# Turned tokens in banks of their own, a new order of VectorE's first work, and fillers at the start of a fused attention and FFN kernel

## The chip, the cores and the metric

The kernel runs on one core of a Trainium2 chip. A core has five engines that run their own instruction streams and meet through semaphores: TensorE (PE, matrix products and transposes), VectorE (DVE), ScalarE (ACT), GpSimd (POOL) and SyncE (SP, which here issues most of the DMA transfers). Matrix products are written to PSUM, a small memory of banks; everything else lies in SBUF. The metric is the time of one execution on the device in microseconds (us), the lower the better, given as the median of several runs.

## The reference

The input x has 4 batches of 512 tokens of 256 features, all in fp32. Cut to what matters:

```python
xn = layernorm(x)                              # (4, 512, 256), no gain
# attention block on xn: 16 heads of 128, 4 key/value heads
Q, K, V = xn @ Wq + bq, xn @ Wk + bk, xn @ Wv + bv
attn = softmax(Q K^T / sqrt(128) + causal mask)
y = gelu((attn @ V) @ Wo + bo)                 # exact gelu
s = layernorm(xn + y) * gamma + beta
# FFN on xn: 2 x 1024 hidden features
gate, up = split(xn @ w_gate_up.T)
g = silu((silu(gate) * up) @ w_down.T)
out = x + s * g
```

## The kernel before

Every product is kept close to fp32 by splitting each operand into a high and a low part and adding three products: high by high, high by low, low by high. A split is a copy with rounding (the high part) and a subtraction (the low part). `product` (L251) issues the three matmuls, at L253, L254 and L255 in that order. `split_psum` (L240) splits a PSUM tile, the high part on ACT (L244), the low part on DVE (L245); `split_sbuf` does the same for weights, on the engines that `load_w` is told: L267 and L269 are the high parts on ACT and POOL, L270 the low part.

The work falls into stages.

**Start.** The four 128-token tiles of x[0] are loaded, and with them the columns of the first weight block for FFN feature blocks f = 0 and f = 1 (`st_first`). PE is given 16 transposes of the identity (`warm_up`, L349). For each token tile `moments` takes mean and variance on DVE, `inverse_root` the power of -0.5 on POOL (L362), and `normed` writes xn on DVE (L379) and sends it to DRAM through SP (L382, `fin_dram`). `normed` takes its tile from the pool tag `u`, which has two buffers: the third xn needs the buffer of the first, and so the end of the first one's transfer.

`transposed` (L387) turns two token tiles at a time: four PE transposes (L395), feature half c by token tile k, into one PSUM tile `pxt`, and then for each feature half a split into `xT`. The first weight block is split by `first_hi` (ACT, L337) and `first_lo` (DVE, L341). `behind(key)` puts what is issued inside it after the last instruction noted under that key, in the order of its engine.

**FFN.** `gate_up_product` (L509) multiplies xT of batch b with the gate and up weights of a feature block f: 12 matmuls of 512 columns, and for (b, f) = (0, 0) 24 of 256 columns, the first 256 tokens before the second, so that they can start when only two token tiles are turned. `gate_silu` (ACT, L535), `gate_times_up` (DVE, L538), `inner_hi` (ACT, L545) and `inner_lo` (DVE, L550) make the hidden activations and their split. `down_product` then fills `pd` for each token tile with the down weights `wd` (split by POOL). `gate` (ACT, L572) takes silu of `pd` into a tile of the tag `gate`, which has two buffers; `gate_scaled` (POOL, L577, once each for gamma and beta) and `gate_shifted` (POOL, L581, adds x) prepare what the end needs, and `gate_out` (SP, L584) writes it to `fin_dram`. The activation of gate_3 goes to the buffer of gate_1, and so waits for gate_1's write to land.

Beside it the weights arrive: `load_w` stages each block in one of two buffers, so a block's load waits for the split of the block before the last. `split_group` (L992, L994) loads the query and output weights on ACT's queue, splits them on POOL into `p` tiles and writes the halves to DRAM (`w_dram`, L1000, L1001), from which they are read back in time.

**Attention.** The last FFN batch and 16 phases of attention are recorded by a planner, the class `Order`, whose tasks have costs and fixed keys; all its instructions bear the line L52.

The order of instructions of each engine outside of `Order` is set by the framework's scheduler, from its own model of time, with `behind` as a constraint. An edit at the start can so move instructions further down. Each engine runs its instructions in the order so fixed. DMAs are issued in the order of their queue, SP's or ACT's; semaphores of eight slots are shared by SP's and ACT's transfers in turn, and the issue of one may wait for the landing of an earlier one.

Of the kernel before, what the change touches and what calls it, by code (L numbers as in the profile page):

```python
# [11 lines left out]
F32 = mybir.dt.float32  # L12
# [6 lines left out]
P = 128  # L19
# [162 lines left out]
def kernel(  # L182
# [20 lines left out]
    nc = tc.nc  # L203

    B, L, D = x.shape
# [3 lines left out]
    G = H // KV  # L209
    INTER = wdT.shape[0]  # L210
    NT = L // P
    ND = D // P
# [6 lines left out]
    work = ctx.enter_context(tc.tile_pool(name="work", bufs=2))  # L219
    rows = ctx.enter_context(tc.tile_pool(name="rows", bufs=4))  # L220
    psum = ctx.enter_context(tc.tile_pool(name="psum", bufs=2, space=PSUM))
    dram = ctx.enter_context(tc.tile_pool(name="dram", bufs=1, space=DRAM))

    pe, dve, act, pool, sp = nc.tensor, nc.vector, nc.scalar, nc.gpsimd, nc.sync
    latest = {}

    @contextmanager
    def behind(*keys):

        with ExitStack() as stack:  # L230
            for k in keys:
                for ins in latest[k]:
                    stack.enter_context(tc.issue_after(ins.ins))
            yield


    def pair(tag, bufs, name, n=512):
        return work.tile([P, 2, n], F32R, tag=tag, bufs=bufs, name=name)

    def split_psum(dst, src, bias=None):  # L240

        hi, lo = dst[:, 0], dst[:, 1]
        if bias is None:
            first = nc.scalar.copy(hi, src)  # L244
            second = nc.vector.tensor_tensor(lo, src, hi.bitcast(F32), ALU.subtract)  # L245
        else:
            first = nc.scalar.activation(hi, src, AF.Identity, bias=bias)
            second = nc.vector.scalar_tensor_tensor(lo, src, bias, hi.bitcast(F32), ALU.add, ALU.subtract)
        return first, second

    def product(out_ap, lhs, rhs, first, last, **kw):  # L251

        pe.matmul(out_ap, lhs[0], rhs[0], start=first, stop=False, **kw)  # L253
        pe.matmul(out_ap, lhs[0], rhs[1], start=False, stop=False, **kw)  # L254
        pe.matmul(out_ap, lhs[1], rhs[0], start=False, stop=last, **kw)  # L255


    mhalf = small.tile([P, NT], F32, name="mhalf")
# [34 lines left out]
    ident = const.tile([P, P], F32, name="ident")  # L293
# [6 lines left out]
    def load_x(b):  # L300
        if b < 2:
            t = work.tile([P, NT, D], F32, tag="xT", bufs=2, name=f"x_{b}")
        else:
            t = p_tiles[NT - 1][:, ts(b - 2, 2)].rearrange("p a n -> p (a n)").rearrange("p (t d) -> p t d", d=D)
        if b > 0:
            nc.sync.dma_start(t, x[b].rearrange("(t p) d -> p t d", p=P))
        return t
# [7 lines left out]
    xs = {0: load_x(0)}  # L315
# [13 lines left out]
    def first_parts(f):  # L329
        v = w_first.rearrange("p s (c u f n) -> p s c u f n", c=ND, u=2, f=2)  # L330
        for c in range(ND):
            yield v[:, 0, c, :, f], v[:, 1, c, :, f], st_first[:, c, :, f]

    def first_hi(f):

        for hi, _, st in first_parts(f):
            nc.scalar.copy(hi, st)  # L337

    def first_lo(f):
        for hi, lo, st in first_parts(f):  # L340
            nc.vector.tensor_tensor(lo, st, hi.bitcast(F32), ALU.subtract)  # L341


    make_identity(nc, ident)


    warm_up = psum.tile([P, P], F32, tag="y0", bufs=1, name="warm_up")
# [4 lines left out]
    mv = small.tile([P, B, NT, 2], F32, name="mv")  # L352
    rstd = small.tile([P, B, NT], F32, name="rstd")

    def moments(dst, src, name):
        st = rows.tile([P, nc.vector.BN_STATS_DIM], F32, tag="st", bufs=4, name=name)
        dve.bn_stats(st, src)
        dve.bn_aggr(dst, st)

    def inverse_root(dst, var):  # L360
        dve.tensor_scalar(dst, var, EPS, 1.0, ALU.add, ALU.mult)
        pool.tensor_tensor(dst, dst, mhalf[:, : dst.shape[1]], ALU.pow)  # L362

    def stats(b, t0, t1):
        for t in range(t0, t1):
            moments(mv[:, b, t], xs[b][:, t], f"st_{b}_{t}")
        inverse_root(rstd[:, b, t0:t1], mv[:, b, t0:t1, 1])
# [7 lines left out]
    w_dram = {(k, g): dram.tile([P, 2, 1024], F32, tag=f"w{k}{g}", name=f"w_dram_{k}{g}") for k in "qo" for g in range(KV)}  # L375

    def normed(b, t):
        xn = work.tile([P, D], F32, tag="u", bufs=2, name=f"xn_{b}_{t}")
        latest["xn"] = (nc.vector.tensor_scalar(  # L379
            xn, xs[b][:, t], mv[:, b, t, 0:1], rstd[:, b, t : t + 1], ALU.subtract, ALU.mult  # L380
        ),)
        nc.sync.dma_start(fin_dram[b][:, t, 0], xn)  # L382
        return xn

    xT = {}

    def transposed(b, t, xn=None):  # L387

        if t == 0:
            xT[b] = [pair("pt", 4, f"xT_{b}_{c}") for c in range(ND)]  # L390
        xn = xn or [normed(b, t), normed(b, t + 1)]
        pt = psum.tile([P, ND, 2, P], F32, tag="s", bufs=2, name=f"pxt_{b}_{t}")
        for c in range(ND):
            for k in range(2):
                nc.tensor.transpose(pt[:, c, k], xn[k][:, ts(c, P)], ident)  # L395
        for c in range(ND):
            dst = xT[b][c][:, :, ds(t * P, 2 * P)]
            latest["xT"] = split_psum(dst, pt[:, c].rearrange("p k q -> p (k q)"))
        if t + 2 == NT:
            for c in range(ND):  # L400
                nc.sync.dma_start(xT_dram[b][:, c], xT[b][c].bitcast(F32))
# [6 lines left out]
    def x_pair(b, c):  # L408
        return xT[b][c][:, 0], xT[b][c][:, 1]

    stats(0, 0, 1)
    stats(0, 1, 2)
    first_hi(0)
    first_xn = [normed(0, t) for t in range(2)]
    with behind("xn"):
        first_lo(0)
        stats(0, 2, 3)
        stats(0, 3, 4)
    transposed(0, 0, first_xn)
    with behind("xT"):  # L420
        first_hi(1)
    transposed(0, 2)
    with behind("xn"):
        first_lo(1)
    wgu = [w_first]


# [40 lines left out]

    banks = [psum.tile([P, L], F32, tag=f"c{r}", bufs=1, name=f"bank{r}") for r in range(G)]

    def h_tiles(b):

# [31 lines left out]
    def gate_up_product(b, f, us=(0, 1)):  # L506
        nonlocal n_ff
        w = wgu[f // 2]
        for u in us:  # L509
            k = n_ff % (G + 2 if b + 1 < B else G)  # L510
            n_ff += 1
            if k < G:
                ps = banks[k]
            else:
                ps = psum.tile([P, L], F32, tag="s", bufs=2, name=f"pg_{b}_{f}_{u}")
            gate_banks.setdefault((b, f), []).append(ps)
        parts = 2 if (b, f) == (0, 0) else 1
        n = L // parts
        for m in range(parts):
            for u in us:  # L520
                for c in range(ND):
                    at = c * 512 + u * 256 + (f % 2) * P
                    hi, lo = x_pair(b, c)
                    product(
                        gate_banks[b, f][u][:, ts(m, n)],
                        (w[:, 0, ds(at, P)], w[:, 1, ds(at, P)]),
                        (hi[:, ts(m, n)], lo[:, ts(m, n)]),
                        m == 0 and c == 0,
                        c == ND - 1,
                        skip_group_check=parts > 1,  # L530
                    )

# [20 lines left out]
    def gate_up(b, f):  # L553
        gate_up_product(b, f)
        gate_silu(b, f)
        gate_times_up(b, f)
        inner_hi(b, f)
        inner_lo(b, f)
# [86 lines left out]
    q0, k0, vr, bank, turned = {}, {}, {}, {}, {}  # L645
# [391 lines left out]
    pe, dve, act, pool, sp = (order.engine(e) for e in (nc.tensor, nc.vector, nc.scalar, nc.gpsimd, nc.sync))  # L1037
# [12 lines left out]
    def group_of(ph):  # L1050
        return divmod(ph, KV)
# [9 lines left out]
    for f in range(NI):  # L1061
        b, key = B - 1, -8.0 + 0.1 * f
        add("Ug", "PE", 1.39, key, lambda b, f: gate_up_product(b, f, (0,)), (b, f), after=[("U", b, f - 1)] + first_queries, takes=BANKS[2 * (f % 2)])
        add("U", "PE", 1.39, key, lambda b, f: gate_up_product(b, f, (1,)), (b, f), after=[("Ug", b, f)], takes=BANKS[2 * (f % 2) + 1])
        add("Us", "ACT", 0.6, key, gate_silu, (b, f), after=[("Ug", b, f)] + first_exps, takes="ctx", mode=2)
        add("Um", "DVE", 0.67, key, gate_times_up, (b, f), after=[("Us", b, f), ("U", b, f)], gives=tuple((t, "U", f) for t in BANKS[2 * (f % 2) :][:2]))
        done = [("D", B - 2, t) for t in range(NT)] if f < 3 else [("U", b, 3)] if f > 3 else []
        add("Uh", "ACT", 0.6, key, inner_hi, (b, f), after=[("Um", b, f), ("Uh", b, f - 1)] + done)
        add("Ul", "DVE", 0.9, key, inner_lo, (b, f), after=[("Uh", b, f)], gives=(("ctx", b, f),))
    order.task(("gb",), "SP", 0.7, -9.0, late_scales, after=[("before",)], takes="ctx", lag=4.5, mode=2)  # L1070
    for b in (B - 2, B - 1):
        e = "POOL" if b + 1 < B else "DVE"
        c = 0.75 if b + 1 < B else 0.35
# [24 lines left out]
    for ph in range(NPH):  # L1098
        b, g = group_of(ph)
# [59 lines left out]
        for i in range(NT):  # L1159
            last = ph + 1 == NPH  # L1160
# [37 lines left out]
        last = ph + 1 == NPH  # L1198
# [47 lines left out]
        if g == KV - 1:  # L1246
# [12 lines left out]
            for t in range(NT):  # L1259
                k = key + (0.1 * (t ^ 2) if late else K["f1"] * t)  # L1260
# [81 lines left out]
```

## Time and profile before

| | |
|---|---|
| median of 3 runs | 621.54 us (620.61 to 622.39) |
| the profiled execution | 621.86 us, span 620.0 us, granted clock 0.994 |
| busy in the span: PE, DVE, ACT, POOL | 608.8, 414.7, 405.5, 452.9 us |
| first transpose of xn on PE, first product | 5.23 us, 6.76 us |
| end of feature blocks 0 and 1 of batch 0 on PE | 17.54 us |
| granted clock of PE from 8.5 to 15.0 us | 0.50 |
| PE idle from 60 to 100, 100 to 140, 140 to 200 us | 1.22, 0.21, 1.10 us |

All times of a profile are counted from the start of the span; the time of the execution is 1.86 us longer than the span. A row of a timeline has the start, the length, the engine, the line of the kernel and the operation with the tiles that it writes and reads, and in brackets how long the engine was idle before it and what released it. The chain of work is followed back from the last instruction: each row has the start and the length, and what the chain passes through there. The rows of windows give each engine's busy time in a stretch, with the number of instructions, then the granted clock, the DMA engines' busy share and their rate.

### The profile page before, as it was taken

What the parts mean: (1) busy time and instruction counts of PE and PEld (TensorE: products, weight loads), DVE (VectorE), ACT (ScalarE), POOL (GpSimd) and SP (SyncE); (2) the same over time, 40 slices, a digit from 0 to 9 for tenths busy, and PEclk for the clock granted to TensorE, in tenths of its full rate; (3) what the DMA queues carried; (4) which work ended last, traced back from release to release, by engine and by line L of the source; (5) the groups of instructions that cost most, each with busy time, mean ns of one, the idle gap of its engine ahead of it and who ended that gap; (6) DMA issues with size and microseconds to landing.
All of it is one profiled execution on the core that took longest, in us unless ns stands there. A gap on an engine that the chain in (4) does not pass through costs nothing.

```text
span 620.0 us, 16073 instructions
## 1 busy us (share of the span) xinstructions
PE 608.8 (98%) x6100; PEld 550.0 (89%) x6100; DVE 414.7 (67%) x1139; ACT 405.5 (65%) x1030; POOL 452.9 (73%) x591
## 2 busy tenths in 40 slices
PE   7999999999999999999999999999999999999997
PEld 6888888898987999899899989898998899998996
DVE  5964545745528876748777774877687569668747
ACT  3542334754349876759888774987796579678762
POOL 2698767493316988739968993896899659888973
PEclk7999999999999999999999999999999999999999
DMA  7764768464597286762786694298396825839562
GB/s 230 254 205 150 271 225 256 169 230 142 138 315 180 69 201 210 181 194 74 256 233 143 268 234 170 59 289 216 121 338 133 263 73 161 236 99 261 140 170 64
DMA packets 86237, 118.10 MB, mean 190 GB/s; under 512 B 5648, under 2 KB 72336, under 8 KB 82064
## 3 DMA queue, kind: packets, MB, share of 16 engines
q1 hardware_dynamic: 81408, 113.93, 62.0%
q10 hardware_dynamic: 4752, 3.15, 1.7%
q8 instruction: 48, 0.79, 0.5%
q14 instruction: 29, 0.24, 0.1%
HBM read 87.70 MB, written 29.36 MB: 189 GB/s over the span
## 4 chain that ended last, share of the span: by engine, by line
PE 80%; POOL 7%; DMA 6%; DVE 4%; issue 1%; ACT 1%; SPq 0%; ACTq 0%; DVEq 0%; POOLq 0%
PE bank L52 42%; PE py L52 14%; PE ps L52 11%; PE pv L52 4%; PE pd L52 3%; PE pk L52 3%; DMA w_dram_o<-p 2%; DVE y L52 1%; POOL w_d L270 1%; DMA st_gu<-in_wguT_dram 1%; DMA st_d<-in_wdT_dram 1%; DMA w_dram_q<-p 1%; DMA fin_dram<-gate 1%; POOL p L52 1%; POOL gate L577 1%
## 5 line engine op out<-in xcount | busy, mean ns | idle before, releaser
L52 POOL TENSOR_SCALAR p<-p,total 128x384 f32<-128x384 f32 (+7 forms) x248 | 119.1, 500 | 28.3 <-DVE total L52 27.4
L52 ACT ACTIVATE p<-p,least 128x192 f32<-128x192 f32 (+15 forms) x256 | 130.6, 512 | 10.7 <-DVE least L52 9.6
L52 POOL TENSOR_TENSOR pT<-u_more,pT 128x512 fp32r<-128x512 f32 x78 | 101.3, 1308 | 26.3 <-ACT pT L52 26.1
L52 PEld LDWEIGHTS bank<-pT,vr 32*128 32x128 f32 x3168 | 113.3, 185 | 6.1 <-issue 1.7
L52 PE MATMUL bank<-pT,vr 32*128 32x256 f32 (+15 forms) x3168 | 118.3, 303 | 0.0
L52 POOL TENSOR_TENSOR pT<-u,pT 128x512 fp32r<-128x512 f32 x82 | 105.6, 1296 | 15.7 <-ACT pT L52 15.5
L52 PE MATMUL py<-w_o,ctxT 128*128 128x256 f32 x768 | 107.0, 285 | 1.3 <-DVE y L52 0.7
L52 PEld LDWEIGHTS py<-w_o,ctxT 128*128 128x128 f32 x768 | 100.9, 191 | 6.6 <-DVE y L52 1.5
L52 DVE CUSTOM_DVE_ANT_0 p<-ps,mask 128x192 f32<-128x192 f32 (+15 forms) x170 | 69.8, 434 | 47.3 <-PE ps L52 46.8
L52 PE MATMUL bank<-xT_again,w_q 128*128 128x512 f32 x384 | 97.4, 394 | 0.8 <-DVE least L52 0.6
L52 PEld LDWEIGHTS bank<-xT_again,w_q 128*128 128x128 f32 x384 | 70.3, 188 | 15.3 <-DVE least L52 1.5
L52 PE MATMUL ps<-kT,qT 128*128 128x352 f32 (+11 forms) x387 | 74.9, 325 | 0.0
L52 ACT ACTIVATE ctxT<-bank,bv_sb 128x512 fp32r<-128x512 f32 (+1 forms) x68 | 42.7, 662 | 48.8 <-PE bank L52 42.6
L52 DVE STREAM_TRANSPOSE u_more<-p 128x512 f32<-128x512 f32 x78 | 53.3, 693 | 21.1 <-POOL pT L52 10.3
L52 DVE STREAM_TRANSPOSE u<-p 128x512 f32<-128x512 f32 x82 | 56.2, 692 | 14.4 <-POOL p L52 8.1
L52 PEld LDWEIGHTS ps<-kT,qT 128*128 128x128 f32 x387 | 60.1, 189 | 5.1 <-issue 0.5
L52 ACT CAST pT<-u_more 128x512 fp32r<-128x512 f32 x78 | 47.6, 618 | 21.9 <-DVE u_more L52 17.4
L52 DVE SCALAR_TENSOR_TENSOR ctxT<-bank,bv_sb,ctxT 128x512 fp32r<-128x512 f32 (+1 forms) x68 | 47.2, 711 | 17.6 <-ACT ctxT L52 17.5
L52 ACT CAST pT<-u 128x512 fp32r<-128x512 f32 x82 | 50.3, 618 | 10.3 <-DVE u L52 9.1
L52 DVE SCALAR_TENSOR_TENSOR qT<-bank,bq_sb,qT 128x384 fp32r<-128x384 f32 x64 | 38.9, 607 | 22.8 <-ACT q L52 20.2
L52 ACT ACTIVATION_READ_ACCUMULATOR p<-p,least 128x1 f32 x256 | 48.1, 188 | 0.0
L52 ACT ACTIVATE qT<-bank,bq_sb 128x384 fp32r<-128x384 f32 x64 | 37.0, 578 | 14.1 <-PE bank L52 13.9
(146 smaller groups left out, 1039.4 us busy)
## 6 DMA issues: line engine op xcount, KB each, us to landing
vr<-v_dram SPq DMA_DIRECT2D x128, 256.0 KB, 5.3
w_q<-w_dram_q SPq DMA_DIRECT2D x15, 1024.0 KB, 7.6
w_o<-w_dram_o SPq DMA_DIRECT2D x15, 1024.0 KB, 9.8
v_dram<-v SPq DMA_DIRECT2D x16, 512.0 KB, 4.3
fin<-fin_dram SPq DMA_DIRECT2D x16, 384.0 KB, 9.1
xT_dram<-xT SPq DMA_DIRECT2D x8, 512.0 KB, 5.8
fin_dram<-gate SPq DMA_DIRECT2D x16, 256.0 KB, 3.3
xT_again<-xT_dram SPq DMA_DIRECT2D x8, 512.0 KB, 6.4
```

The lines of the kernel that those rows point to most:

```text
L52: made = getattr(self.engine, name)(*args, **kw)
L270: lo_on.tensor_tensor(dst[1], src, dst[0].bitcast(F32), ALU.subtract)
L577: pool.tensor_tensor(g[:, 1 + k], g[:, 0], gb_sb[:, k], ALU.mult)
```

## The change

Only the first batch is touched in the source.

1. `transposed` writes the two feature halves of batch 0 into PSUM tiles of their own, for the first two token tiles under the tag `s`, for the other two under `y0` and `y1`.
2. DVE's first work is reordered: the moments of token tile 2 come before the first split of xT; those of tile 3, one `inverse_root` for both tiles (one POOL instruction in place of two) and the low part of block 1's weights after it; and then xn of tiles 2 and 3, which now take buffers of the tag `gate`.
3. Feature blocks 0 and 1 are both computed in two halves of 256 tokens, and for batch 0 the three partial products go in the order high by high, low weight by high x, high weight by low x.
4. Four transposes of the identity follow the first two token tiles' transposes on PE, three more follow the second.

```diff
-    def product(out_ap, lhs, rhs, first, last, **kw):
...
+    def product(out_ap, lhs, rhs, first, last, parts=((0, 0), (0, 1), (1, 0)), **kw):
+        for k, (i, j) in enumerate(parts):
+            pe.matmul(out_ap, lhs[i], rhs[j], start=first and k == 0, stop=last and k == 2, **kw)
...
     def normed(b, t):
-        xn = work.tile([P, D], F32, tag="u", bufs=2, name=f"xn_{b}_{t}")
+        if (b, t // 2) == (0, 1):
+            xn = work.tile([P, 3, D], F32, tag="gate", bufs=2, name=f"xn_{b}_{t}")[:, 0]
+        else:
+            xn = work.tile([P, D], F32, tag="u", bufs=2, name=f"xn_{b}_{t}")
...
-        pt = psum.tile([P, ND, 2, P], F32, tag="s", bufs=2, name=f"pxt_{b}_{t}")
+        if b == 0:
+            tags = (("s", 2), ("s", 2)) if t == 0 else (("y0", 1), ("y1", 1))
+            pts = [psum.tile([P, 2, P], F32, tag=g, bufs=n, name=f"pxt_{b}_{t}_{c}") for c, (g, n) in enumerate(tags)]
+        else:
+            both = psum.tile([P, ND, 2, P], F32, tag="s", bufs=2, name=f"pxt_{b}_{t}")
+            pts = [both[:, c] for c in range(ND)]
         for c in range(ND):
             for k in range(2):
-                nc.tensor.transpose(pt[:, c, k], xn[k][:, ts(c, P)], ident)
+                latest["pxt"] = (nc.tensor.transpose(pts[c][:, k], xn[k][:, ts(c, P)], ident),)
...
     first_xn = [normed(0, t) for t in range(2)]
     with behind("xn"):
         first_lo(0)
-        stats(0, 2, 3)
-        stats(0, 3, 4)
+        moments(mv[:, 0, 2], xs[0][:, 2], "st_0_2")
     transposed(0, 0, first_xn)
+    with behind("pxt"):
+        for _ in range(4):
+            nc.tensor.transpose(banks[G - 1][:, :P], ident, ident)
     with behind("xT"):
         first_hi(1)
+        moments(mv[:, 0, 3], xs[0][:, 3], "st_0_3")
+        inverse_root(rstd[:, 0, 2:4], mv[:, 0, 2:4, 1])
+        first_lo(1)
     transposed(0, 2)
-    with behind("xn"):
-        first_lo(1)
+    with behind("pxt"):
+        more = psum.tile([P, P], F32, tag="s", bufs=2, name="warm_up_more")
+        for _ in range(3):
+            nc.tensor.transpose(more, ident, ident)
...
-        parts = 2 if (b, f) == (0, 0) else 1
+        parts = 2 if b == 0 and f < 2 else 1
...
+                        ((0, 0), (1, 0), (0, 1)) if b == 0 else ((0, 0), (0, 1), (1, 0)),
```

In the order that the scheduler makes of this, the instructions of every engine differ up to some 115 us. Among them: on SP the writes of xn of tiles 2 and 3 stand behind the loads of the third weight block and of x[2] and x[3]; on PE the first two matmuls with the down weights stand seven matmuls of 512 columns earlier; on POOL the addition of x to gate_1 (L581) stands behind the two multiplications of gate_2 (L577) in place of ahead of them; on ACT the activation of gate_0 of batch 1 (L572) stands ahead of the issue of the DMAs that load the fourth block of query weights (L992). From about 115 us on the order of PE is the same in both.

## The prediction, made before the changed kernel was run

> **What bounds the kernel now.** I read the page first, then windows, then the chain that ended last.
>
> ```profile
> PE 608.8 (98%) x6100; PEld 550.0 (89%) x6100; DVE 414.7 (67%) x1139; ACT 405.5 (65%) x1030; POOL 452.9 (73%) x591
> ...
> PE 80%; POOL 7%; DMA 6%; DVE 4%; issue 1%; ACT 1%; SPq 0%; ACTq 0%; DVEq 0%; POOLq 0%
> ```
>
> TensorE (PE) is busy 98% of the span, yet a fifth of the chain is not PE. The windows (columns: PE, PEld, DVE, ACT, POOL busy, then granted clock, DMA share, GB/s) show where.
>
> ```profile
> 5.00:8.50 3.50, 2.29 (x14) 1.52 (x13) 2.75 (x12) 1.48 (x5) 1.31 (x3) 1.00 0.77 233
> 8.50:12.00 3.50, 3.04 (x13) 2.27 (x12) 2.07 (x6) 0.68 (x3) 0.00 (x0) 0.50 0.99 274
> 12.00:15.50 3.50, 3.50 (x13) 2.98 (x13) 2.97 (x8) 1.38 (x3) 0.00 (x0) 0.53 1.03 335
> 15.50:18.00 2.50, 2.50 (x16) 2.16 (x15) 1.31 (x7) 1.66 (x4) 1.02 (x1) 1.00 1.07 383
> ...
> 60.00:100.00 40.00, 38.78 (x216) 33.14 (x216) 18.38 (x28) 13.66 (x28) 26.95 (x32) 1.00 0.70 243
> ...
> 200.00:600.00 400.00, 399.32 (x4649) 366.35 (x4651) 287.53 (x849) 306.16 (x807) 326.23 (x422) 1.00 0.65 184
> ```
>
> PE has gaps and half its clock from 8.5 to about 15.3; then none idle until it loses 1.22 us between 60 and 100. From 200 on it is full, and the change leaves that order alone, so a shift of PE reaches the end unless something absorbs it earlier. What could is in the chain, which from 11 to 85 us does not run through PE at all:
>
> ```profile
> 20.55 5.79 DMA st_d<-in_wdT_dram
> 26.43 1.89 POOL w_d L269 x2
> 28.32 3.06 POOL w_d L270 x2
> ...
> 57.05 0.71 POOL gate L581
> 57.77 4.38 DMA fin_dram<-gate
> 62.25 0.38 ACT gate L572
> ...
> 68.01 0.33 DVE xT L245
> ...
> 82.89 1.30 POOL p L270
> 84.21 0.55 ACTq L992
> 84.86 0.39 ACT gate L572
> 85.30 0.38 PE pd L253
> ```
>
> The reader is to see three points where PE can meet POOL, ACT or a DMA however early it comes: w_d at 26.4 to 28.3, gate_3's activation at 62.25, and the first down matmul at 85.30. There alone PE pays:
>
> ```profile
> PE pd L253 <- ACT gate L572: 1.0, 1, 1.0
> ```
>
> **The first 17.5 us.** PE's timeline puts the first product at 6.76, idles of 0.56 at 7.82 (for VectorE's xT) and 0.46 at 11.53 (for ACT's xT), and the end of feature blocks 0 and 1 at 17.54. Two banks remove the 1.09 us that ACT's second copy waits for VectorE's subtract. The reorder takes w_gu lo of block 1 (9.39 to 10.14) to right behind its high half; its blocks land at 7.52 and 7.96, and one ACT cast and one DVE subtract of 0.41 each make it about 8.9. In exchange xn_2 (8.41) comes after that, one aggregate and one rstd of VectorE (0.2 each) and one POOL power (1.06 for two, so about 0.5), with the handovers: about 10.1, and xn_3 10.4. That is paid by block 1's first half: PE now has 24 matmuls of 256 columns before it needs xn_2.
>
> Low case, the clock drops as before at 8.48 until 15.31. Spacing in the timeline is 0.119 us (full) and 0.21 (half). Some 12 of the 24 end by 8.5, the rest take 12 x 0.21 = 2.6, so 11.0; four transposes 0.84, three fillers 0.63, so 12.4, by when xT's high half (0.43 after the transposes) is there; 24 second-half matmuls are 14 to 15.31 and 10 x 0.119 more: 16.5. Gain 1.0. The 512-column matmuls cut in two cost nothing, 2 x 0.119 against 0.2275. High case, full clock throughout: xn_3 sets the start at about 11.5, then 24 x 0.119 gives 14.4; the next block needs w_gu1's low half, which DVE ends at 15.6 as now (x[1] lands at 12.94 and stands ahead), so at most 2.2 gain. The four first fillers cost 0.43 before the first product, in time PE waited for ACT's copy (0.46 idle). If uncovered, 0.4.
>
> Which case? The clock changed at 5.07 (the warm-up's transposes go from 0.22 to 0.11 apart), 8.48 and 15.31, spaced by multiples of 3.41; in 5.07 to 8.48 PE was busy 65% and lost it, and 8.48 to 11.89 at 86% did not bring it back. After, the first of these is nearly full, the second has a hole waiting for xn_2. I keep both ends, 1.0 and 2.2.
>
> The warm-up's 16 transposes, 1.81 to 5.34 with nothing else, were followed by the full clock at 5.07: here fillers count. The Trainium skill ("TensorE: Matmul & The Clock Gate", Part 4) says against this change that transposes do not count as busy for the clock; by that rule the low case would hold and the sum below would be the same, since the next step absorbs either.
>
> SP: the writes of xn_2 and xn_3 (256 KB) move behind st_gu2 and the last x loads; at the 335 GB/s of that window st_gu2 lands 0.78 earlier. ScalarE's w_gu2 (16.28) and POOL's (16.98) follow; PE first needs them at 21.6, so that is hidden. The bytes ahead of st_d0 are the same and the queue's share is about 1.0, so st_d0 I leave at 26.34; bound: none to 0.78 earlier. beta, the small biases and bo move on the same queue; nothing reads them before 45.
>
> **26 to 30 us.** In the changed order the first two matmuls with w_d0 stand seven 512-column matmuls earlier (45 of them before it, against 64, of which 12 are block 1's). PE would come there at 29.84 - 7 x 0.2275 - 1.0 = 27.25 or sooner; POOL's first w_d0 cast ends near 27.7. So PE waits 0.5 to 1.7 there and leaves 27.75 + 1.6 = 29.35 in place of 29.84: **-0.5 in both cases**. The early gain is mostly spent here.
>
> **57 to 70 us.** POOL's add of x to gate_1 is now behind both multiplies of gate_2:
>
> ```profile
> 57.01 0.74 POOL L581 TENSOR_TENSOR gate<-gate,x 128x256 f32<-128x256 f32 x1
> 57.70 1.89 POOL L577 TENSOR_TENSOR gate<-gate,gb_sb 128x256 f32<-128x256 f32 x2
> ```
>
> It ends 1.9 later, so its write on SP starts near 59.7 instead of 57.77, ahead of xn_2, gate_2 and xn_3. gate_3 takes gate_1's buffer and waits for that write to land (62.15); behind gate_3 on ACT's queue stand h and hq of the next batch, and behind them DVE's xT lo (68.01 to 68.34), which PE reads at 68.83: 0.44 of slack. If D is how much later the write lands, PE's shift there becomes the larger of -0.5 and D - 0.44. D lies between 0 and 2.0 (4.38 us to land, kept). The write of before did not take 4.38 by itself: st_o, 512 KB, was issued at 57.08 and landed at 61.48, and the DMA share was 1.00 from 60 to 63. A gate write alone took 2.0 (88.63 to 90.59), so from 59.7 at the earliest 61.7. Behind st_o, 256 KB at that window's 365 GB/s are 0.7: 62.2. I take D = 0.3: shift **-0.14**.
>
> **85 us.** On ACT, the activation of gate_1_0 now precedes st_q3's DMA issue (84.21), which waits for POOL's p. The 1.0 that PE waited at 85.30 goes; next is hq, 0.2, which I leave. **-1.0**; bounds 0 (ACT still late) and -1.2.
>
> **115 us.** PE waited 0.2 for POOL's k (115.28), behind w_dram_o's write of 5.29 us from 109.70. PE earlier by 1.1 brings that write's source earlier, since it follows PE through qT, but the queue is full there; I charge **+0.2**, bounds 0 and 1.1. Nineteen more PE instructions are seven fillers and twelve halves, counted above.
>
> Sum: -0.14 - 1.0 + 0.2 = **-0.9**. The profiled execution took 621.86 (span 620.0), so 620.9; the median of the runs shown is 0.32 below it, so **620.6**.
>
> **Rivals.** About 0.3%, 1.86 us, is what a measurement of this kernel tells from no change.
>
> *A, the gain is kept.* st_d0 lands 0.78 earlier, POOL's unbroken chain from there to 60 moves with it, gate_1's write lands 0.4 before 62.15: -0.84 at 69, -1.0 at 85, nothing at 115: -1.85, 619.7 by the median; 0.8 more if k and p follow on. For: DMA share only 0.74 from 18 to 30. Against: 5.79 us of that landing is queue. 0.27.
>
> *B, slower.* gate_1's write keeps its 4.38 us: D = 2.0, +1.56 at 69. From D = 1.24 the end is later than before. At worst, gate_3's later multiplies on POOL push p and st_q, st_o by 1.9 down to k at 115, and nothing of the 1.0 is recovered: +1.9, 623.4; with the 1.0 recovered, 622.3. For: four writes issue within 1.7 us (those of xn_2, gate_2 and xn_3 at 60.84, 60.43 and 61.38). Against: the full-rate queue above. 0.2.
>
> *C, the change doesn't do what it says:* the clock drops all the same and the fillers only take PE time, 0.4, or the 1.0 wait at 85 remains. The w_d0 meeting covers the first, the second gives +0.1: 621.6. 0.13.
>
> **How the numbers follow.** The likeliest, 0.4, is 620.6, by D from 0 to 1 between 620.3 and 621.3. A reaches down to 618.9, B up to 623.4. Leaving out the outer part of each: 618.9 to 623.3. Faster by over 0.3%: most of A, 0.26. Slower by over 0.3%: B's worst half and surprises at the start, 0.13. The rest, 0.61, within.
>
> **What would show it.** End of blocks 0 and 1 at 15.3 to 16.5; a PE wait of 0.5 to 1.7 for POOL w_d near 27.7; POOL's add at about 59; gate_3's activation at 62.3 to 62.8 (64.2 is B); no PE wait near 85. I am wrong if w_d0's cast starts well before 26.4, or if PE pays a wait over 1 us between 65 and 71.

## The result, and the profile after

The changed kernel takes 623.69 us in the median of 19 runs (620.41 to 626.86), the kernel before beside it 621.54 us (620.6 to 623.22); the ratio is 1.0034 (95% interval 1.0018 to 1.0050). It is slower by a third of a percent, where 620.6 us was forecast and 623.3 was the upper end of the range. The runs of the changed kernel also lie further apart. Its profiled execution took 624.08 us, with a span of 622.3.

The first lines of its page:

```profile
PE 609.1 (98%) x6119; PEld 550.8 (89%) x6119; DVE 417.0 (67%) x1138; ACT 405.8 (65%) x1030; POOL 450.9 (72%) x590
...
PE 72%; DMA 11%; POOL 10%; DVE 4%; issue 2%; SPq 1%; ACT 0%; ACTq 0%; POOLq 0%; DVEq 0%
```

PE's share of the chain has fallen from 80 to 72%, and DMA's and POOL's have grown: the chain now leaves PE for longer. The windows, in the same columns as before:

```profile
5.00:8.50 3.50, 3.48 (x24) 2.68 (x23) 3.36 (x11) 1.76 (x5) 0.31 (x1) 1.00 0.73 221
8.50:12.00 3.50, 3.19 (x25) 2.72 (x24) 1.82 (x7) 1.11 (x4) 0.70 (x1) 1.00 0.97 307
12.00:15.50 3.50, 3.50 (x26) 3.15 (x25) 2.72 (x9) 0.75 (x3) 0.00 (x0) 1.00 0.96 270
...
18.00:30.00 12.00, 10.63 (x50) 8.35 (x49) 12.00 (x31) 6.34 (x12) 6.13 (x7) 1.00 0.83 268
...
60.00:100.00 40.00, 40.00 (x229) 34.97 (x228) 21.36 (x32) 15.47 (x32) 27.64 (x34) 1.00 0.73 248
100.00:140.00 40.00, 36.87 (x216) 33.48 (x215) 22.19 (x58) 23.05 (x57) 26.10 (x42) 0.96 0.63 213
```

The start does what it was to do: from 5.0 to 15.5 us PE idles for 0.33 us in place of 1.67, at full clock. From 60 to 100 PE is busy without a break (38.78 before). But from 100 to 140 it idles for 3.13 us and its mean clock is 0.96. PE's waits of this kernel (us in all, times, longest; from 0 to 30 and from 100 to 140 us) say on whom:

```profile
PE pd L254 <- POOL w_d L268: 1.4, 1, 1.4
...
PE ps L52 <- POOL k L52: 3.1, 1, 3.1
```

The first was forecast. The second is the first score product of the attention, which needs k0, a sum that POOL makes; before, it waited 0.2 there. Set one profile against the other, instruction by instruction (start after minus start before), and the lead of PE reads as follows: 2.75 us at 23 us; 0.40 from 45 to 65; 1.34 at 82; 2.58 from 86 to 113; then, with the first score at 116.08 in place of 115.75, PE is 0.33 us behind, and 1.70 behind from 122 on, to 2.45 at 600. So 2.6 us had been won by 113 us, and 2.91 of the shift go in one wait. The other 1.37 go in the four microseconds behind it. PE's timeline there:

```profile
111.35 1.60 PE L52 MATMUL pd<-w_d,hw 128*128 128x256 f32 x12
116.08 0.66 PE L52 MATMUL ps<-k,q 128*128 128x32 f32 x4 [3.13 <-POOL k L52]
...
118.08 1.69 PE L52 MATMUL ps<-kT,qT 128*128 128x256 f32 x6
119.57 1.00 PE L52 MATMUL bank<-kT,qT 128*128 128x320 f32 x3
120.37 1.71 PE L52 MATMUL ps<-kT,qT 128*128 128x352 f32 x6
```

and three of the same groups before:

```profile
115.75 0.66 PE L52 MATMUL ps<-k,q 128*128 128x32 f32 x4 [0.21 <-POOL k L52]
...
117.91 1.02 PE L52 MATMUL ps<-kT,qT 128*128 128x256 f32 x6
...
119.21 1.16 PE L52 MATMUL ps<-kT,qT 128*128 128x352 f32 x6
```

The same six products of 256 columns take 1.69 us in place of 1.02: half clock, for one stretch of about 3.4 us. Windows of the changed kernel confirm it (the last three numbers are clock, DMA share, GB/s):

```profile
116.10:118.40 2.30, 2.30 (x18) 2.29 (x19) 1.65 (x13) 1.64 (x9) 0.15 (x1) 0.94 0.00 1
118.40:121.80 3.40, 3.40 (x15) 3.40 (x15) 2.15 (x10) 3.04 (x12) 0.50 (x2) 0.54 0.01 2
121.80:124.00 2.20, 2.20 (x13) 2.02 (x12) 2.02 (x9) 1.94 (x6) 0.75 (x3) 1.00 0.00 0
```

By the trace's own record of the clock the stretch goes from 118.1 to 121.5.

Why did k not come earlier with PE? The chain of the changed kernel has it:

```profile
97.90 3.00 POOL p L269 x2
100.90 0.02 issue
100.92 7.70 DMA st_o<-in_wo_dram
...
109.36 1.06 POOL p L268
...
110.43 4.90 DMA w_dram_o<-p
115.33 0.02 issue
115.37 0.07 issue
115.44 0.18 POOL p L297
115.61 0.43 POOL k L52
```

k0 itself needs only kT. But POOL runs in order, and ahead of k0 stand the memsets that clear the p tiles for the scores (L297), each behind the landing of the last weight dump that used its tile. That dump follows the last block of output weights, st_o. Its load was issued 1.02 us earlier than before (100.92 for 101.94), yet it landed 0.54 later (108.62 for 108.08), while the DMA engines were fully taken (a share of 1.07 from 101.0 to 108.6): the writes of xT and of w_dram_q, issued 2.4 and 2.0 us earlier than before, share them with it. So the chain to k is bound by transfers, and PE's lead runs into it. In the kernel before, POOL stood in the same order:

```profile
108.23 1.20 POOL L269 TENSOR_SCALAR p<-st_o 128x512 fp32r<-128x512 f32 x2 [0.51 <-DMA st_o<-in_wo_dram]
...
115.10 0.18 POOL L298 MEMSET p<- 128x96 f32 x1 [0.51 <-DMA w_dram_o<-p]
115.24 0.46 POOL L52 TENSOR_TENSOR k<-kT 128x128 f32<-128x128 f32 x1
```

Five profiles, this one and four of the experiments below, have the changed order up to here and k on POOL. In them PE is 0.70 to 2.58 us ahead of the kernel before at 113 us, and k starts between 1.31 earlier and 0.95 later than there, so it does not move with PE.

### The profile page after: what moved, and what is told of

Its sections match the earlier page's. It is cut to its first block, busy times and chain, and to the rows that moved or that the text cites. A ratio compares the mean times of both kernels' runs of the same rounds, so it can differ in the third digit from the quotient of the medians.

```text
span 622.3 us, 16106 instructions
## 1 busy us (share of the span) xinstructions
PE 609.1 (98%) x6119; PEld 550.8 (89%) x6119; DVE 417.0 (67%) x1138; ACT 405.8 (65%) x1030; POOL 450.9 (72%) x590
## 4 chain that ended last, share of the span: by engine, by line
PE 72%; DMA 11%; POOL 10%; DVE 4%; issue 2%; SPq 1%; ACT 0%; ACTq 0%; POOLq 0%; DVEq 0%
PE bank L52 39%; PE py L52 12%; PE ps L52 10%; PE pv L52 4%; PE pd L52 3%; PE pk L52 3%; DMA w_dram_o<-p 2%; DMA vr<-v_dram 1%; POOL p L52 1%; POOL pT L52 1%; DMA st_o<-in_wo_dram 1%; DMA xT_dram<-xT 1%; DMA w_dram_q<-p 1%; DMA x<-in_x_dram 1%; POOL gate L592 1%
## 5 line engine op out<-in xcount | busy, mean ns | idle before, releaser
L52 POOL TENSOR_TENSOR pT<-u,pT 128x512 fp32r<-128x512 f32 x82 | 105.7, 1296 | 15.7 <-ACT pT L52 15.5
L52 PEld LDWEIGHTS py<-w_o,ctxT 128*128 128x128 f32 x768 | 101.0, 190 | 6.5 <-DVE y L52 1.5
L52 PEld LDWEIGHTS bank<-xT_again,w_q 128*128 128x128 f32 x384 | 70.2, 188 | 15.5 <-DVE least L52 1.5
L254 PE MATMUL bank<-xT,w_gu 128*128 128x512 f32 (+1 forms) x216 | 48.9, 370 | 0.0
```

Of the source, the lines that this page charges most:

```text
L52: made = getattr(self.engine, name)(*args, **kw)
L254: pe.matmul(out_ap, lhs[i], rhs[j], start=first and k == 0, stop=last and k == 2, **kw)
```

## The experiments

Theory 1: the lead is real, and is lost at the first score, to POOL's k and then to half clock. Theory 2: the loss lies elsewhere, and the wait is only where it shows. All ratios are to the kernel before, run beside them on the same chip, where its median was 622.3 to 622.6.

**k0 on VectorE, in the changed kernel and in the kernel before.** The order of all other instructions stays.

```diff
-        pool.tensor_tensor(k0[b, g], k[:, 0], k[:, 1], ALU.add)
+        (pool if b or g else dve).tensor_tensor(k0[b, g], k[:, 0], k[:, 1], ALU.add)
```

> The changed kernel with one edit: the sum that makes k0 of the first attention phase is taken by VectorE in place of POOL, so it no longer stands behind POOL's clears of the p tiles. The order of every engine is else the same. Theory 1 (the lead of 2.6 us that PE has at 113 us is lost at the first score product, which waits 3.1 us for POOL's k, behind the landings of w_dram_o, and then pays 1.4 us for a clock that the idle time halved): PE goes on near 113, and meets at the latest the clears of p tile 1 (113.8); no half clock after 116; median 619 to 621.3, spread of the runs about that of the kernel before (2.6 us). Theory 2 (the loss lies elsewhere, and the wait would come an instruction or two later all the same): 623 to 624.5, with a wait of some 3 us at another instruction by 120 us.

> The kernel before with the same single edit (k0 of the first phase on VectorE). Theory 1: PE came there only 0.2 to 0.4 us before k, so no more than that is to be had: 621.1 to 621.6. Theory 2 says the same of this one; it is the control that the edit by itself is worth little: if it gains over 1 us, the edit and not the lead is what the first run shows.

Measured: the changed kernel with the edit 619.84 us (619.11 to 621.0, five runs), ratio 0.9957 (0.9945 to 0.9968): faster than both kernels. The kernel before with it 622.23 us, ratio 0.9990 (0.9979 to 1.0001). PE's timeline and the windows of the first:

```profile
112.03 1.60 PE L52 MATMUL pd<-w_d,hw 128*128 128x256 f32 x12
113.61 0.63 PE L52 MATMUL ps<-k,q 128*128 128x32 f32 x4
```

```profile
112.00:116.00 4.00, 4.00 (x34) 3.81 (x32) 3.07 (x15) 2.53 (x11) 2.03 (x8) 1.00 0.63 240
116.00:118.00 2.00, 2.00 (x14) 1.91 (x13) 1.91 (x12) 2.00 (x10) 0.09 (x1) 1.00 0.01 4
118.00:122.00 4.00, 4.00 (x27) 3.73 (x26) 3.89 (x16) 3.71 (x14) 2.84 (x8) 1.00 0.00 0
```

The score follows the product before it without a gap, PE stays full, the clock too, and the wait does not come back at a later instruction: PE is 1.91 us ahead of the kernel before at 113 us, and 1.97 after 600. The edit is worth 0.10% where PE has no lead and 0.77% where it has one (the ratios 1.0034 and 0.9957, from two chips). Theory 2 falls.

**The wait filled with PE work.** In the function of the score products, ahead of the first:

```diff
+            if (b, g, t) == (0, 0, 0):
+                for _ in range(26):
+                    pe.transpose(ps[:, :P], ident, ident)
```

and, as a second form, 12 matmuls of 512 columns in place of the 26 transposes.

> The changed kernel with one edit: 26 transposes of the identity (about 2.8 us) stand on PE ahead of the first score product, in the PSUM tile that it writes, so PE works through the wait for POOL's k. Order else the same. Theory 1: the first score comes at 116.1 as in the changed kernel, the wait is there, but the clock stays full behind it: 1.4 us less than the profiled 624.1 and near 622.0 in the median, with the runs closer together than 620.4 to 626.9. Rival (the half clock after the wait costs nothing that counts, or transposes do not hold it): 623.2 to 624.2, half clock between 118 and 122 as now.

> The changed kernel with 12 matmuls of 512 columns (about 2.7 us) on PE ahead of the first score product, in the PSUM tile that it writes, in place of 26 transposes; order else the same. Theory 1 with the clock (a wait that leaves PE idle for 3 us is followed by half clock, and that counts at the end): ratio 1.0005 to 1.002, clock about 1.0 and the runs closer together. Rival (the clock after the wait is not what counts in the median, as the transposes suggest): 1.003 to 1.005 again.

Measured: 624.85 us, ratio 1.0041 (1.0020 to 1.0061), and, in six runs, 624.95 us, ratio 1.0039 (1.0021 to 1.0058): no gain, against theory 1's numbers. Yet in both profiles the half clock at 118 us is gone, with transposes in the wait as with matmuls. The time is lost at another place: 0.7 us at about 534, for which the profile names nothing,

```profile
PE bank L52 <- issue: 1.1, 2, 0.7
```

(PE's waits from 200 us on, of the kernel with transposes) and half clock from 536.6 to 540.1 in both, over 2 us of shift there. No kernel without added PE instructions at 113 us shows that stall. So these two could not tell the theories apart. What the stall is was not shown. Two things in the traces point to PE's instructions coming late, which no run here tests: the first PE instruction behind it is the 10177th record of matmuls and weight loads in both, though one kernel has 28 such records more ahead of the score than the other; and a transfer of 16 KB on the queue that loads instructions starts 2.6 and 2.5 us before PE goes on.

**The fillers left out, and the wait filled with few instructions.** First the changed kernel without its seven fillers; then the same with three plain fp32 matmuls of 512 columns ahead of the first score, which keeps PE at fewer instructions than the changed kernel:

```diff
-    with behind("pxt"):
-        for _ in range(4):
-            nc.tensor.transpose(banks[G - 1][:, :P], ident, ident)
...
+            if (b, g, t) == (0, 0, 0):
+                for _ in range(3):
+                    pe.matmul(ps, ident, mask, start=True, stop=True)
```

> The changed kernel without its seven filler transposes; the order of every engine is else the same. Theory 1: the first stage may lose its full clock (half from 8.5 to 15.3, blocks 0 and 1 ending 1 to 2 us later), but PE still comes to w_d0 before POOL has it, so nothing changes from 28 us on: 623.2 to 624.2. Rival (the fillers bring their own loss or gain to the end): off by over 0.7 us. If the clock is full without them, the fillers did nothing.

> The changed kernel without its seven fillers at the start, and with 3 plain fp32 matmuls of 512 columns on PE ahead of the first score product, in the PSUM tile that it writes; each should take four passes of 0.23, so about 2.7 us in all. PE has fewer instructions than in the changed kernel, so a stall that comes from the place of the instructions in the stream (the 0.7 us near 534 in both earlier fillings) should not come. Theory 1 with the clock: half clock after the idle wait is most of what the changed kernel loses, so with the wait filled the runs have a clock nearer 1.0 and the ratio is 0.9995 to 1.0015. Rival (the clock does not count): 1.002 to 1.004 as without these matmuls.

Measured: without fillers 624.63 us (621.56 to 625.66), ratio 1.0021 (1.0005 to 1.0038), above the 624.2 that was expected at most, but by the ratio no slower than the changed kernel; with the wait filled 622.92 us (621.84 to 624.33), ratio 1.0005 (0.9993 to 1.0018). PE's timeline of the second:

```profile
111.66 1.60 PE L52 MATMUL pd<-w_d,hw 128*128 128x256 f32 x12
113.10 2.74 PE L52 MATMUL ps<-mask,ident 128*128 128x512 f32 x6
115.86 0.66 PE L52 MATMUL ps<-k,q 128*128 128x32 f32 x4
...
117.86 1.01 PE L52 MATMUL ps<-kT,qT 128*128 128x256 f32 x6
```

The score comes at 115.86, about as late as in the changed kernel, but the six products of 256 columns take 1.01 us again. The mean granted clock of each run says the same over all runs. A stretch of 3.4 us at half clock costs 1.7 us of 620, that is 0.0027 of the mean clock. Without fillers the ten runs have 0.997 (four) and 0.995 (six), none 1.0; with the wait filled they have 1.0 (seven of twelve, 621.8 to 623.2 us) and 0.997 (five, 623.3 to 624.3 us). One stretch at half clock is taken away, and with it 1.0 us by the two ratios, 1.7 by the two medians. In the 19 runs of the changed kernel too the time follows the clock: 620.4 to 622.4 us at 0.999 and 1.0, 622.2 to 624.7 at 0.997, 623.5 to 625.8 at 0.994 and 0.995, 626.9 at 0.991 and 0.992; 0.65 us for each 0.001. So half clock is the larger part of what the changed kernel loses against the kernel before in the median, some 2 us; the wait for k takes the lead that had been won. (The two kernels without fillers were run on different chips, each beside the kernel before, and their intervals overlap.)

The fillers at the start did nothing that can be seen: in its one profile the kernel without them keeps the full clock in the first stage. Windows of it:

```profile
5.07:8.48 3.41, 3.16 (x20) 2.41 (x20) 3.27 (x12) 1.70 (x5) 0.17 (x1) 1.00 0.74 218
8.48:11.89 3.41, 2.76 (x22) 2.30 (x21) 1.73 (x7) 1.08 (x4) 0.70 (x1) 1.00 0.94 275
```

In that one execution the first score came at 114.44 after a wait of 1.0, which was not followed by half clock at 118; there was a stretch of it at 187 instead. It is the fastest of the ten.

**Where the lead comes from: ACT's order in the kernel before.** The loads of st_q3 are put behind the activation of gate_1_0, as the changed kernel has it; PE, DVE and SP keep their order. Once so, and once with k0 on VectorE too.

```diff
-        act.activation(g[:, 0], downs[b, t], AF.Silu)
+        latest["gate", b, t] = (act.activation(g[:, 0], downs[b, t], AF.Silu),)
...
-                    split_group(*splits[b, f])
+                    with behind(*[("gate", 1, 0)] * ((b, f) == (2, 5))):
+                        split_group(*splits[b, f])
```

> The kernel before with one edit: on ACT the activation of gate_1_0 (and one cast beside it) stands ahead of the issue of st_q3's loads, as it does in the changed kernel; on POOL the x-add of gate_1_0 moves up one place with it; PE, DVE and SP keep their order. Theory 1 (the 2.6 us of lead at 113 us come mostly from this, not from the start): the wait of 1.0 us at 85 goes, PE comes to the first score 1 to 2 us earlier and there waits 1.2 to 2.2 us for POOL's k; the end is not earlier, between the time before and 1.5 us above it (ratio 0.999 to 1.0025). Rival (the lead comes from the start): PE comes to the first score within 0.4 us of the kernel before.

> The same edit of the kernel before, and k0 of the first phase on VectorE. No part of the change at the start is in it. Theory 1: the lead passes the first score, so 1.0 to 2.2 us less than before: ratio 0.9965 to 0.9985. Rival (the start brings the gain of the changed kernel with k0 on VectorE): no better than k0 alone on the kernel before, 0.9985 to 1.0.

Measured: 622.36 us, ratio 0.9995 (0.9982 to 1.0008); with k0 on VectorE 621.83 us, ratio 0.9990 (0.9979 to 1.0002). The second is no better than k0 on VectorE alone, so theory 1's number for it was missed and the rival's fits. In both profiles PE's shift against the kernel before improves by 1.24 us at 85 us, but only the second shows the swap at work: there PE comes to that place with the kernel before (0.07 us ahead at 83) and leaves it 1.31 ahead. In the first it comes 1.44 late and leaves 0.20 late, and the kernel before with k0 on VectorE, which has ACT's old order, does the same (1.38 and 0.13): whoever is late there has nothing left to wait for. PE's waits from 60 to 112 of the first kernel show one that made it late:

```profile
PE pd L253 <- ACT hq L545: 0.9, 1, 0.9
```

The first score starts at 116.24 us in the one profile (115.75 in the kernel before, so 0.5 later) and at 114.09 in the other, where no wait precedes it; there 1.3 us are lost again to half clock from 187 to 191. So the swap alone makes a lead in one profile of two, and over the runs nothing clear of noise.

**The halves of block 1 undone.** `parts` is 2 for f = 0 alone again; from about 52 us on ACT and POOL then have the order of the kernel before, while the banks, VectorE's order and the fillers stay. Once so, and once with k0 on VectorE. With them, the changed kernel without fillers and with k0 on VectorE.

```diff
-        parts = 2 if b == 0 and f < 2 else 1
+        parts = 2 if (b, f) == (0, 0) else 1
```

> The changed kernel with feature block 1 in whole products of 512 columns again; the two banks, VectorE's order and the fillers stay. With it ACT's order of gate_1_0 and st_q3, and POOL's of gate_1's x-add, come back to those of the kernel before. Theory 1: PE is 0.5 to 2.5 us ahead at 20 us, -0.5 to 0.2 at 60, waits about 1 us near 85 as before, and comes to the first score at most 1 us ahead; ratio 0.9985 to 1.001. Rival (the edits at the start cost time by themselves): 1.002 or more.

> The changed kernel with feature block 1 in whole products (and so ACT's and POOL's order of the kernel before) and k0 of the first phase on VectorE. Theory 1 (the lead at the first score comes from the new order between 60 and 85 us more than from the start): less is gained than with the halves, ratio 0.997 to 0.999. Rival (the lead comes from the start alone): 0.9945 to 0.9965.

> The changed kernel without its seven fillers, with k0 of the first phase on VectorE. Theory 1 (the fillers at the start do nothing that reaches the end, since PE waits for w_d0 in any case): the ratio of the changed kernel with k0 on VectorE again, 0.9945 to 0.997. Rival (fillers hold the clock and that is worth something): 0.998 or more.

Measured: without the halves 622.36 us, ratio 0.9998 (0.9982 to 1.0013), and with k0 on VectorE 621.62 us, 0.9981 (0.9964 to 0.9997). Without fillers and with k0 on VectorE 620.44 us, 0.9965 (0.9952 to 0.9979). In the first, PE came to the score 1.74 us ahead of the kernel before, not at most 1, and waited 0.8 us; that did not cost it half clock. It was 1.37 ahead at 60 us, after a wait of 0.4 for w_d, where "-0.5 to 0.2" was expected, and its wait near 85 was 0.2 and not 1. So the edits at the start do no harm by themselves that could be seen. With the halves and the order that comes with them the kernel is 0.36% slower as it stands, and 0.16 to 0.24% faster once k0 is out of POOL's queue. Where the lead is made shows in the shifts. In the seven profiles with the halves (the changed kernel's, and six with edits at the fillers, at k0 or at 113 us) PE is 0.99 to 3.25 us ahead at 18 us, between 0.40 ahead and 1.28 behind from 60 to 65, and gains 1.83 to 2.30 from there to 86. In the two without them it is 1.37 and 1.38 ahead at 60 to 65, and 1.74 and 0.05 at 86. The intervals of 0.9957 and 0.9965 overlap, so the fillers are again not told from nothing.

## Why the prediction was wrong

The step that failed is the one at 115 us. The prediction put: PE waits 0.2 for k; an earlier PE brings the write's source earlier; "I charge +0.2, bounds 0 and 1.1". Measured in the profiled executions: 2.91 us of shift lost in the wait (from 2.58 ahead to 0.33 behind), and 1.37 by half clock behind it, +4.3 in all where 1.1 was the bound. Two things were wrong in it. The chain to k was taken to follow PE through qT, when it follows the landing of st_o and of POOL's dumps, in a full queue, and POOL's order puts k0 behind them. The chain before showed POOL's memset directly ahead of k. It also put VectorE's qT, done at 108.77, ahead of POOL's second cast of st_o, but the two casts ran on from 108.23, 0.15 after st_o had landed, so that link was a near tie. And a wait was priced at its length alone. A wait can also be followed by 3.41 us at half clock. In these profiles that happened behind this one of 3.13 us and behind one of 1.12 for w_d (without fillers, k0 on VectorE; half clock from 27.9 to 31.3), and not behind waits of 1.7 for w_d (k0 on VectorE) or 1.04 and 0.83 for k. The profile before, with PE 65% busy from 5.07 to 8.48 and half clock behind it, showed that small waits can be enough, and the prediction used it there and not here.

- The first 17.5 us: 15.3 to 16.5 was forecast for the end of blocks 0 and 1; their last products end near 14.9, with two products of the next block among them. The clock stayed full, and w_gu's low half came at 7.87 to 8.61 (8.9 forecast), xn_2 at 9.73 (10.1). The mechanism was right and the size too small; most of it is spent at the next step.
- 26 to 30 us: a wait of 0.5 to 1.7 for w_d near 27.7 and a shift of -0.5 were forecast; the wait was 1.4, at 27.13, and the shift from 45 on is -0.40. Right in this profile; in the six others with the halves the shift there is -0.13 to 1.28.
- 57 to 70 us: POOL's add and gate_1's write came late as forecast, and the write was not late in landing. In POOL's timeline, and ACT's for gate_3:

```profile
57.53 1.44 POOL L592 TENSOR_TENSOR gate<-gate,gb_sb 128x256 f32<-128x256 f32 x2
58.92 1.94 POOL L596 TENSOR_TENSOR gate<-gate,x 128x256 f32<-128x256 f32 x2
```

```profile
62.23 0.38 ACT L587 ACTIVATE gate<-pd 128x256 f32<-128x256 f32 x1 [0.48 <-DMA fin_dram<-gate]
```

  The write was issued at 60.14 and landed at 62.13, in 1.99 us in place of 4.38, which fits the prediction's argument that the load of st_o ahead of it had made it long. D is 0 (0.3 taken). Rival B, which rested on a long landing, did not happen, though the sign of the result was its sign.
- 85 us: -1.0 was forecast. The shift goes from -0.40 at 65 to -2.58 at 86: 0.94 between 65 and 82, where the kernel before has a number of short stalls on PE (0.40 at 77.6 the longest) that the new order does not have, and 1.24 at 85. So the term at 85 was nearly right; what the prediction put at nothing, without a reason, are the 0.94 us ahead of it, and with them PE met k with a lead of 2.58 where 1.1 had been counted.
- Rival A, the gain kept, came nearest to the size of the lead (1.85 for 2.58), but by luck: its cause, st_d0 landing 0.78 earlier, did not come (POOL's first cast of w_d starts at 26.45, 26.43 before), nor its -0.84 at 69 (-0.32). A lead that is kept is what the kernel does once k0 is on VectorE: 619.84 us on a chip on which the kernel before takes 622.56. With k0 on POOL its "nothing at 115" was wrong.
- The fillers: of the filler transposes the prediction said that they count for the clock. The first stage keeps its clock without them, so at the start that stays open; at 113 us 26 transposes stood in the wait, and in that profile the clock stayed full behind them, which speaks for it. The Trainium skill ("TensorE: Matmul & The Clock Gate", Part 1) has it that the clock is judged in free-running windows of 3.4 us, so that a kernel's phase to them varies from run to run. The half-clock stretch at 118.1 to 121.5 has that length, the 13 profiles here come to full clock first between 4.8 and 11.0 us, and the spread of the changed kernel's runs goes with their clock, which agrees.

What stays open: how many of the half-clock stretches in runs without a profile lie behind the wait for k, and how many at 187 to 192, where other kernels here had one; the stall at 534 us; how long a wait must be to bring half clock behind it; and by how much single edits at the start would count in another order, since the scheduler moves later work with each of them.

## What to carry to other kernels

When PE is given a lead, follow it to the first product that needs something from a chain of transfers, and read on that engine's queue what stands ahead of the operation that PE will wait for: an operation that has its inputs but stands behind clears that wait for DMAs is late for no need, and moving it to another engine turned a loss of 0.34% into a gain of 0.43%. Price a wait on PE at its length and, from about a microsecond up, as a chance at up to 1.7 us more for the clock behind it. And look at the order of all engines after an edit at the start: here the lead was made between 65 and 86 us, some 60 us behind the lines that were changed.

## What the runs showed of the hardware that was not expected

The start of the kernel before had half clock from 8.5 to 15.3 us in its profile and in that of the kernel before with k0 on VectorE, and full clock in two other profiles with the same first instructions (those with ACT's order changed); these were 1.76 and 2.37 us ahead at 18 us, and 0.29 and 1.09 at 45. Three plain fp32 matmuls of 512 columns took 2.74 us, 0.91 each, and show as two instructions apiece. A transfer of 256 KB whose landing took 4.38 us behind another took 1.99 when issued 2.4 us later, and landed at the same time.
